# Value projections of a decoder layer: two pairs of groups by seven block products, and eight multiplications of a constant at the start

## The chip, the cores and the metric

The kernel runs on one core of a Trainium2 chip. A core has five engines that run side by side, each with its own queue of instructions, which it works off in order: TensorE (PE in the profile, with its weight loads shown apart as PEld) multiplies matrices into PSUM, VectorE (DVE), ScalarE (ACT) and GpSimd (POOL) work on elements, and SyncE (SP) does nothing here but issue transfers. Sixteen DMA engines move data between HBM and SBUF. The engines wait for each other by semaphores. The metric is the device time of the program in microseconds, from first to last instruction; smaller is better. Everything is computed in float32.

## The reference

One decoder layer over 8 sequences of 112 tokens with 512 features: causal self-attention with 16 heads of 128, linear cross-attention to a context, and a mixture of eight experts of which each token takes two, each followed by a layernorm. The change touches the self-attention alone:

```python
q = jnp.einsum('bsd,hed->bhse', x, W_Q)
k = jnp.einsum('bsd,hed->bhse', x, W_K)
v = jnp.einsum('bsd,hed->bhse', x, W_V)
scores = jnp.einsum('bhse,bhme->bhsm', q, k) * scale
scores = jnp.where(causal, jnp.float32(-1000000000.0), scores)
pattern = jax.nn.softmax(scores, axis=-1)
z = jnp.einsum('bhsm,bhme->bhse', pattern, v)
out = jnp.einsum('bhse,hde->bsd', z, W_O)
```

## The kernel before

**Tiles.** The 896 tokens are 7 tiles of 128 (`xn`, tokens on the partitions). TensorE turns each tile with four transposes (`transposing`, L199), and VectorE or ScalarE copies the result from PSUM to `xT`, features on the partitions. The weights come as blocks of 1 MB, each for a group of four heads (512 columns), into nine buffers `slab[0]` to `slab[8]`. The names in the profile are `slab`, `xn`, `x0T` (for `xT`), `vps` (PSUM of a value product), `qk_5a` (PSUM of the projections of head 5), `ws` (combined weights), `xs` (combined tokens).

**Seven products.** `seven` (L304) computes two matrix products with the same right side at once. The two weight blocks and the tokens are split in halves, by features (`low`, `high`) and by tokens (sequences 0 to 3 and 4 to 7). Four products of halves for each of the four blocks of the result would be eight; with sums and differences of the halves it is seven. The sums of the weights are ws[0] = w2 low + w2 high, ws[1] = ws[0] - w1 low, ws[2] = w1 low - w2 low, ws[3] = w1 high - ws[1]. The sums of the tokens are made once (`combine_tokens`, L289) and called s1 to s4 below (`xs[:, 0]` to `xs[:, 3]`): three subtractions on VectorE (L293 to L295), s3 on GpSimd (L292). `seven` uses three PSUM banks a, b and c; into a and c products are added on after ScalarE (L328, L332, L335, L339) or VectorE (L330, L336, L342) has read what stood there. Each of the seven is two multiplications of 128 rows.

**Values.** Head group 0 and group 3 have their values projected directly (`project_v`, L344): 8 sequences, four multiplications each, 32 in all. Groups 1 and 2 are done as a pair (`project_v_pair`, L363): four times fourteen multiplications, 56 in all. Group 0 comes first of everything, each sequence as its tile is turned; the pair comes in step h = 4 of the loop over heads, group 3 in step h = 8. `v_buf` holds the values of two groups.

**The loop over heads.** In step h the queries and keys of head h are projected (by `seven`, with its combined weights on GpSimd, L299 to L302), mixed with the transposes and products of head h - 1 (`mix`), followed by the scores of head h and their softmax (`patterns`): scaling on ScalarE (L419), the mask on GpSimd (L425), row maximum (L435) and shift (L436) on VectorE, exponential on ScalarE (L437), row sum (L439), reciprocal and scaling on VectorE. After every fourth head, the output of the group is projected and added to `xn` (L261, L268).

**Order.** The order of the instructions on each engine is set by a scheduler that the program calls on while it is built; what it places depends on its costs, not on the order of the text. Each engine then runs its queue strictly in that order. Loads from SP's queue also stand in order; the program counts the transfers of SP and ScalarE with eight semaphores in turn, so that a ninth transfer waits for the first.

Of the kernel before, what the change touches and what calls it, by code (L numbers as in the profile page):

```python
# [17 lines left out]
ORDERED = {ET.PE, ET.DVE, ET.Activation, ET.SP}  # L18

P = 128  # L20
B, S, D = 8, 112, 512
T = B * S
NT = T // P
# [3 lines left out]
G = 4  # L27
# [33 lines left out]
def decoder_layer(ctx: ExitStack, tc: tile.TileContext, t_in: dict, out: bass.AP):  # L61
# [13 lines left out]
    def bank(name: str, tag: str = "mm"):  # L75
        return psum.tile([P, 512], F32, tag=tag, name=name)
# [3 lines left out]
    def weights(which: str, i: int, at: int):  # L80

        w = slab[at]
        nc.sync.dma_start(out=w.rearrange("p c n -> p (c n)"), in_=t_in[which][i])
        return w
# [1 line left out]

    xe = keep.tile([P, NT, W], F32, tag="xn", name="xn")
    xn = xe[:, :, :D]
    wv0 = slab[0]
    nc.scalar.dma_start(out=xn[:, 0, :], in_=t_in["x"][:P, :])  # L90
    for c in range(C):
        nc.sync.dma_start(out=wv0[:, c, :], in_=t_in["wv"][0][:, c * 512 : (c + 1) * 512])
    for t in range(1, NT):
        nc.sync.dma_start(out=xn[:, t, :], in_=t_in["x"][t * P : (t + 1) * P, :])

    ident = const.tile([P, P], F32, name="ident")
    make_identity(nc, ident)
# [39 lines left out]
    for half in range(2):  # L137
# [5 lines left out]
            allow_small_or_imprecise_dtypes=True,  # L143
        )
    place.append(pairs_.rearrange("p i q e -> p (i q) e"))
    nc.gpsimd.iota(
        xe[:, :, XK],
        pattern=[[P, NT]],
        base=0,
        channel_multiplier=1,  # L150
        allow_small_or_imprecise_dtypes=True,
    )

    upto = counting("upto", [P, NT + 1, E], [[0, NT + 1], [T, E]])

# [40 lines left out]
                in_=blank[:, :D].unsqueeze(1).broadcast_to([P, 2 * NT + 1, D]),  # L196
            )

    def transposing(xT, name: str):  # L199

        for t in range(NT):
            ps = bank(f"{name}_ps{t}")
            for c in range(C):
                nc.tensor.transpose(
                    ps[:, c * P : (c + 1) * P], xn[:, t, c * P : (c + 1) * P], ident
                )
            src = ps.rearrange("p (c n) -> p c n", c=C)
            if t % 2:
                nc.scalar.copy(xT[:, :, t * P : (t + 1) * P], src)
            else:  # L210
                nc.vector.tensor_copy(xT[:, :, t * P : (t + 1) * P], src)  # L211
            yield t
# [57 lines left out]


    xT = keep.tile([P, C, T], F32, tag="xT", name="x0T")
    turned = transposing(xT, "x0T")
    with tc.tile_pool(name="att", bufs=2) as att:


# [9 lines left out]
        )  # L286
        v_buf = [att.tile([S, B, 512], F32, name=f"v{i}", bufs=1) for i in range(2)]

        def combine_tokens():  # L289
            b11, b12 = xT[:, low, :HALF], xT[:, low, HALF:]  # L290
            b21, b22 = xT[:, high, :HALF], xT[:, high, HALF:]
            nc.gpsimd.tensor_sub(xs[:, 2], b22, b12)  # L292
            nc.vector.tensor_sub(xs[:, 0], b12, b11)  # L293
            nc.vector.tensor_sub(xs[:, 1], b22, xs[:, 0])
            nc.vector.tensor_sub(xs[:, 3], b21, xs[:, 1])  # L295

        def combine_weights(out, w1, w2):

# [5 lines left out]
        def seven(name: str, tag: str, w1, w2, ws, cols, turned_: bool, c11, c12, c21, c22):  # L304

            x = [xs[:, i, :, cols] for i in range(4)]
            b11, b21, b22 = xT[:, low, cols], xT[:, high, cols], xT[:, high, HALF:]
            b22 = b22[:, :, cols]
            rows, n = (S, 512) if turned_ else (P, HALF)

            def product(ps, a, b_, start: bool):

                for c in range(C // 2):
                    l, r = (b_, a) if turned_ else (a, b_)
                    nc.tensor.matmul(  # L315
                        ps[:rows, :n],
                        l[:, c, :],
                        r[:, c, :],
                        start=start and c == 0,
                        stop=c == C // 2 - 1,  # L320
                        skip_group_check=not start,
                    )

            e1, e2 = ends[:rows, 0, :n], ends[:rows, 1, :n]
            pa, pb, pc = (bank(f"{name}{i}", tag) for i in "abc")
            u, r, q = (ps[:rows, :n] for ps in (pa, pb, pc))
            product(pa, w1[:, low], b11, True)
            nc.scalar.copy(e1, u)  # L328
            product(pb, w1[:, high], b21, True)
            nc.vector.tensor_add(c11, e1, r)  # L330
            product(pa, ws[1], x[1], False)
            nc.scalar.copy(e2, u)  # L332
            product(pc, ws[0], x[0], True)
            product(pa, ws[2], x[2], False)
            nc.scalar.copy(e1, u)  # L335
            nc.vector.tensor_add(c22, e1, q)  # L336
            yield
            product(pa, w2[:, high], x[3], False)
            nc.scalar.copy(c21, u)  # L339
            yield  # L340
            product(pc, ws[3], b22, False)
            nc.vector.tensor_add(c12, e2, q)  # L342

        def project_v(g: int, w):  # L344
            for b in range(B):
                next(turned, None)
                if b == 1:
                    next(turned, None)
                ps = bank(f"vps_{g}_{b}")
                for c in range(C):  # L350
                    nc.tensor.matmul(  # L351
                        ps[:S, :],
                        xT[:, c, b * S : (b + 1) * S],
                        w[:, c, :],
                        start=(c == 0),
                        stop=(c == C - 1),
                    )
                if b % 2:
                    nc.scalar.copy(v_buf[g % 2][:, b, :], ps[:S, :])
                else:  # L360
                    nc.vector.tensor_copy(v_buf[g % 2][:, b, :], ps[:S, :])

        def project_v_pair(g: int, w1, w2, ws):  # L363

            v1, v2 = v_buf[g % 2], v_buf[(g + 1) % 2]
            pieces = None
            for b in range(B // 2):
                last, pieces = pieces, seven(
                    f"vps_{g}_{b}",
                    ("mm", "aux")[b % 2],  # L370
                    w1,
                    w2,
                    ws,
                    slice(b * S, (b + 1) * S),
                    True,
                    v1[:, b],
                    v1[:, b + B // 2],
                    v2[:, b],
                    v2[:, b + B // 2],
                )  # L380
                for _ in pieces:
                    pass

        def project_qk(h: int, wq, wk, qk):
            hl = slice(h % G * DH, (h % G + 1) * DH)
# [82 lines left out]
                )  # L468
                yield

        project_v(0, wv0)
        combine_tokens()
        at_qk = ((4, 5), (0, 3), (4, 5), (0, 3))
        at_o = (6, 7, 6, 2)
        pats = None
        for h in range(NH + 1):
            g = h // G
            qk = {}
            if h < NH:
                if h % G == 0:  # L480
                    wq, wk = (weights(n, g, i) for n, i in zip(("wq", "wk"), at_qk[g]))
                if h == 0:
                    wv1, wv2 = weights("wv", 1, 1), weights("wv", 2, 2)
                if h == 1:
                    turn_biases()
                if h % G == 2:
                    wo = weights("wo", g, at_o[g])
                if h == 2 * G - 1:
                    wv3 = weights("wv", 3, 1)
                if 2 <= h < E + 3:  # L490
                    clear(h - 2)
            project = project_qk(h, wq, wk, qk) if h < NH else iter(())
            mixed = mix(h - 1, pats) if h else iter(())
            next(project, None)
            next(mixed, None)
            next(project, None)
            next(mixed, None)
            next(mixed, None)
            next(project, None)
            for _ in mixed:  # L500
                pass
            if h < NH:
                pats = patterns(h, qk)
            if h % G == 0 and h:
                if h == G:
                    ws = [slab[i].rearrange("p (a c) n -> p a c n", a=2) for i in (4, 5)]
                    nc.gpsimd.tensor_add(ws[0][:, 0], wv2[:, low], wv2[:, high])
                    nc.gpsimd.tensor_sub(ws[0][:, 1], ws[0][:, 0], wv1[:, low])
                    nc.vector.tensor_sub(ws[1][:, 0], wv1[:, low], wv2[:, low])
                    nc.vector.tensor_sub(ws[1][:, 1], wv1[:, high], ws[0][:, 1])  # L510
                    project_v_pair(1, wv1, wv2, [ws[0][:, 0], ws[0][:, 1], ws[1][:, 0], ws[1][:, 1]])
                elif h == 2 * G:
                    project_v(3, wv3)
                for t in project_and_add(zT, wo, f"ops_{h}"):
                    if h == NH:
                        layernorm(t, "ln1")
# [4 lines left out]
    rb = const.tile([P, E], F32, name="rb")  # L521
    nc.scalar.dma_start(out=rb, in_=t_in["rb"].partition_broadcast(P))
    rows = const.tile([P, NT, 2], I32, name="rows")

    def route(t: int):

# [906 lines left out]
```

## Time and profile before

The median of three runs is 978.79 us (977.5 to 979.02).

| | before |
|---|---|
| median of 3 runs | 978.79 us |
| the profiled execution: its time | 978.09 us |
| its span | 976.5 us |
| matmul records of TensorE | 3915 |
| busy: VectorE / ScalarE / GpSimd | 502.6 / 247.3 / 206.1 us |
| value products of group 0 begin / the first head's projections begin | 7.13 / 40.74 us |
| the h = 4 step's pair begins, head 5's projection begins | 109.21, 188.38 us |
| the h = 8 step's values begin, head 9's projection begins | 240.30, 298.54 us |
| data moved by DMA | 130.48 MB |

A profile is one execution. Its times are positions from the start of its span; the span is shorter than the time by what lies around it (1.6 us). A float32 multiplication stands in it as two records. The times of single matmul records overlap, as they are pipelined, so the distance between their starts counts, not their length. The loads at the start, in 2 us windows: 3, 235, 356, 309, 273, 369, 424, 422, 430 GB/s up to 18 us.

### The profile page before, as it was taken

How to read it: one execution, taken by the hardware profiler on the slowest of the kernel's cores; microseconds unless marked ns; L12 is line 12 of the kernel's file. 1: busy time of each engine (PE TensorE's matmuls, PEld its weight loads, DVE VectorE, ACT ScalarE, POOL GpSimd, SP SyncE). 2: the span in 40 equal slices, each digit the busy share in tenths (PEclk: the TensorE clock that was granted, in tenths of full speed). 3: DMA queues.
4: the chain of work that ended last, by engine and by line, in shares of the span. 5: the costliest groups of instructions: out<-in, count | busy, mean ns of one | idle time of the engine just before them, and what ended most of it. 6: DMA issues, size and time to landing. Idle time of an engine off the chain costs nothing. (4 is left out here: it accounts for less than half of the span.)

```text
span 976.5 us, 11044 instructions
## 1 busy us (share of the span) xinstructions
PE 920.5 (94%) x3915; PEld 467.9 (48%) x3915; DVE 502.6 (51%) x1117; ACT 247.3 (25%) x429; POOL 206.1 (21%) x267
## 2 busy tenths in 40 slices
PE   7998999999999999999999999997969999999981
PEld 3465644466445564664554445454544443334440
DVE  1356521145312552456430756677558864556785
ACT  1133311033102330332322233322224322222232
POOL 3133300021101230302002212212102332222343
PEclk9999999999999999999999999999979999999997
DMA  8995004102011001021100111112356899768953
GB/s 339 348 349 210 1 1 172 44 0 87 1 44 43 1 1 43 1 89 60 32 1 1 32 33 54 54 55 69 143 212 258 282 366 371 270 240 342 386 180 133
DMA packets 35063, 130.48 MB, mean 134 GB/s; under 512 B 3862, under 2 KB 8022, under 8 KB 25152
## 3 DMA queue, kind: packets, MB, share of 16 engines
q1 hardware_dynamic: 29296, 114.01, 32.0%
q0 software_dynamic: 4768, 14.98, 4.3%
q10 hardware_dynamic: 944, 0.79, 0.3%
q8 instruction: 31, 0.51, 0.2%
q14 instruction: 24, 0.20, 0.1%
HBM read 122.02 MB, written 30.06 MB: 156 GB/s over the span
## 5 line engine op out<-in xcount | busy, mean ns | idle before, releaser
L1143 PE MATMUL gups<-slab,bT 128*64 128x512 f32 (+1 forms) x416 | 134.1, 602 | 1.2 <-DMA slab<-in_wu_dram 1.2
L261 PE MATMUL ops<-slab,zT 128*128 128x512 f32 x224 | 97.9, 593 | 0.0
L1143 PEld LDWEIGHTS gups<-slab,bT 128*64 128x64 f32 (+1 forms) x416 | 49.1, 160 | 69.5 <-issue 67.4
L299 POOL TENSOR_TENSOR ws<-slab 128x256 f32<-128x256 f32 x16 | 11.6, 727 | 281.1 <-PE qk_5c L315 83.0
L1172 PE MATMUL yps<-slab,aT 128*64 128x512 f32 (+1 forms) x208 | 68.2, 601 | 0.9 <-ACT aT L1044 0.7
L261 PEld LDWEIGHTS ops<-slab,zT 128*128 128x128 f32 x224 | 42.0, 190 | 50.3 <-issue 49.5
L351 PE MATMUL vps<-slab,x0T 128*112 128x512 f32 x128 | 59.4, 619 | 1.0 <-DVE x0T L211 0.8
L1151 DVE TENSOR_TENSOR gu<-gups,biases 128x512 f32<-128x512 f32 x36 | 24.8, 689 | 59.5 <-PE gups L1143 59.5
L268 DVE TENSOR_TENSOR xn<-xn,ops 128x512 f32<-128x512 f32 x28 | 19.2, 685 | 55.3 <-PE ops L261 55.2
L1044 ACT COPY aT<-aT_ps 128x512 f32<-128x512 f32 x18 | 10.5, 585 | 133.5 <-PE aT_ps L1040 133.4
L1172 PEld LDWEIGHTS yps<-slab,aT 128*64 128x64 f32 (+1 forms) x208 | 24.8, 160 | 37.7 <-issue 35.2
L466 DVE COPY zT<-zps 128x448 f32<-128x448 f32 x32 | 20.0, 624 | 39.8 <-PE zps L459 39.8
L459 PEld LDWEIGHTS zps<-pT,v 112*128 112x128 f32 x256 | 33.5, 192 | 12.3 <-issue 11.2
L351 PEld LDWEIGHTS vps<-slab,x0T 128*112 128x112 f32 x128 | 23.0, 185 | 31.7 <-issue 30.0
L435 DVE TENSOR_REDUCE nm<-p 112x4 f32<-112x448 f32 x32 | 19.7, 615 | 30.5 <-POOL p L425 30.5
L261 PE MATMUL xops<-slab,gate 128*128 128x512 f32 x56 | 27.4, 635 | 7.1 <-DVE gate L870 7.1
L459 PE MATMUL zps<-pT,v 112*128 112x112 f32 x256 | 33.4, 273 | 0.0
L587 POOL DMA_INDIRECT store<-xn,rows x14 | 14.0, 1000 | 82.5 <-DVE count L627 58.8
L1185 POOL DMA_INDIRECT parts<-y,nums x16 | 16.9, 1056 | 62.6 <-DVE y L1183 48.6
L995 DVE STREAM_SHUFFLE biases<-biases 128x1024 f32<-128x1024 f32 (+1 forms) x28 | 30.0, 1104 | 0.0
L419 ACT ACTIVATE p<-sps 112x448 f32<-112x448 f32 x32 | 17.4, 543 | 45.6 <-PE sps L411 45.6
L411 PE MATMUL sps<-k,q 128*112 128x112 f32 x256 | 28.0, 262 | 0.0
(816 smaller groups left out, 1676.6 us busy)
## 6 DMA issues: line engine op xcount, KB each, us to landing
slab<-in_wg_dram SPq DMA_DIRECT2D x26, 1024.0 KB
slab<-in_wu_dram SPq DMA_DIRECT2D x26, 1024.0 KB
slab<-in_wd_dram SPq DMA_DIRECT2D x26, 1024.0 KB
store<-slab SPq DMA_DIRECT2D x8, 1806.0 KB
cT<-in_ctxT_dram SPq DMA_DIRECT2D x8, 750.0 KB
slab<-in_wq_dram SPq DMA_DIRECT2D x4, 1024.0 KB
slab<-in_wk_dram SPq DMA_DIRECT2D x4, 1024.0 KB
slab<-in_wo_dram SPq DMA_DIRECT2D x4, 1024.0 KB
```

Of the source, the lines that this page charges most:

```text
L261: nc.tensor.matmul(ps, aT[:, c, t * P : (t + 1) * P], w[:, c, :], start=(c == 0), stop=(c == C - 1),)
L268: nc.vector.tensor_add(xn[:, t, :], xn[:, t, :], ps)
L351: nc.tensor.matmul(ps[:S, :], xT[:, c, b * S : (b + 1) * S], w[:, c, :], start=(c == 0), stop=(c == C - 1),)
L411: nc.tensor.matmul(ps[:S, i * S : (i + 1) * S], qk["q"][:, rows], qk["k"][:, rows], start=True, stop=True,)
L419: nc.scalar.activation(p.rearrange("s b m -> s (b m)"), ps[:S, :HALF], AF.Copy, scale=1.0 / math.sqrt(DH),)
L435: nc.vector.tensor_reduce(nm, p, AX.X, ALU.max, negate=True)
L459: nc.tensor.matmul(zps[:, i * S : (i + 1) * S], v[:, half * 4 + i, hl * DH : (hl + 1) * DH], pT[:, i * S : (i + 1) * S], start=True, stop= ...
L466: nc.vector.tensor_copy(zT[:, hl, half * HALF : (half + 1) * HALF], zps[:, :HALF])
L995: nc.vector.stream_shuffle(b, b, [0] * XH)
L1143: nc.tensor.matmul(ps[rows_], st["bT"][:, c, rows_], slab[3 * q + k][:, c, :], start=(c == 0), stop=(c == C - 1),)
L1151: nc.vector.tensor_add(a, ps, st["bias"][:, k * I : (k + 1) * I])
L1172: nc.tensor.matmul(ps[rows_], st["aT"][:, c, rows_], slab[3 * q + 2][:, c, :], start=(c == 0), stop=(c == C - 1 and s < STEPS - 1),)
```

## The change

Values of groups 0 and 1 are now a pair at the very start, and groups 2 and 3 a pair in step h = 8; step h = 4 has no value products, and `project_v` is gone. For the first pair both weight blocks are loaded at the start, in halves of 512 KB, and the tiles in the order 0, 1, 3, 4, 5, 2, 6: wv1, tiles 1, 3, 4, 5, then wv2, then tiles 2 and 6. The blocks for the second pair are loaded in step h = 5. `combine_tokens` is called twice, for the first two and the last two of the four batches. The weights of a pair are combined by `combine_values`: on VectorE, only ws[2] of the first pair on GpSimd. The start stands in a block in which the queues of TensorE, VectorE, ScalarE and SP keep the order of the text; GpSimd's is left to the scheduler. At its head TensorE multiplies a tile of ones by itself eight times.

```diff
+    load_tile(0, nc.scalar)
+    for half in range(2):
+        load_half(wv1, 0, half)
+    for t in tiles[1:5]:
+        load_tile(t)
+    for half in range(2):
+        load_half(wv2, 1, half)
+    for t in tiles[5:]:
+        load_tile(t)
...
-            if t % 2:
+            if t % 2 or t and tiles != range(NT):
                 nc.scalar.copy(xT[:, :, t * P : (t + 1) * P], src)
...
             nc.vector.tensor_add(c11, e1, r)
+            if turned_:
+                yield
...
+        def combine_values(w1, w2, at, engine=nc.vector):
+
+            ws = [slab[i].rearrange("p (a c) n -> p a c n", a=2)[:, a] for i in at for a in (0, 1)]
+            nc.vector.tensor_add(ws[0], w2[:, low], w2[:, high])
+            engine.tensor_sub(ws[2], w1[:, low], w2[:, low])
+            nc.vector.tensor_sub(ws[1], ws[0], w1[:, low])
+            nc.vector.tensor_sub(ws[3], w1[:, high], ws[1])
+            return ws
...
-        project_v(0, wv0)
-        combine_tokens()
+        with tc.manual_schedule(engines=ORDERED):
+
+            warm = bank("warm", "aux")
+            for _ in range(8):
+                nc.tensor.matmul(warm[:, :P], allones, allones, start=True, stop=True)
+            turn = lambda n: list(itertools.islice(turned, n))
+            turn(1)
+            ws = [slab[i].rearrange("p (a c) n -> p a c n", a=2)[:, a] for i in (2, 3) for a in (0, 1)]
+            first_values = project_v_pair(0, wv1, wv2, ws)
+            next(first_values[0])
+            turn(2)
+            combine_values(wv1, wv2, (2, 3), nc.gpsimd)
+            next(first_values[1])
+            turn(2)
+            combine_tokens(0, 2 * S)
+            turn(2)
+        for pieces in first_values[:2]:
+            for _ in pieces:
+                pass
+        combine_tokens(2 * S, HALF)
+        for pieces in first_values[2:]:
+            for _ in pieces:
+                pass
...
-                if h == 0:
-                    wv1, wv2 = weights("wv", 1, 1), weights("wv", 2, 2)
...
-                if h == 2 * G - 1:
-                    wv3 = weights("wv", 3, 1)
+                if h == G + 1:
+                    wv1, wv2 = weights("wv", 2, 1), weights("wv", 3, 2)
...
-                if h == G:
-                    ws = [slab[i].rearrange("p (a c) n -> p a c n", a=2) for i in (4, 5)]
-                    nc.gpsimd.tensor_add(ws[0][:, 0], wv2[:, low], wv2[:, high])
-                    nc.gpsimd.tensor_sub(ws[0][:, 1], ws[0][:, 0], wv1[:, low])
-                    nc.vector.tensor_sub(ws[1][:, 0], wv1[:, low], wv2[:, low])
-                    nc.vector.tensor_sub(ws[1][:, 1], wv1[:, high], ws[0][:, 1])
-                    project_v_pair(1, wv1, wv2, [ws[0][:, 0], ws[0][:, 1], ws[1][:, 0], ws[1][:, 1]])
-                elif h == 2 * G:
-                    project_v(3, wv3)
+                if h == 2 * G:
+                    for pieces in project_v_pair(2, wv1, wv2, combine_values(wv1, wv2, (0, 3))):
+                        for _ in pieces:
+                            pass
```

The `iota` that numbers the tokens moves from the head of the program to the text behind the attention. The orders of the queues named in the prediction are those of the two built programs.

More of the change, by code (lines that the diff above doesn't have):

```diff
@@ L88, in decoder_layer, with load_tile, load_half @@
     xn = xe[:, :, :D]
[L89 to L94, printed above, removed]
+    wv1, wv2 = slab[0], slab[1]
+    tiles = (0, 1, 3, 4, 5, 2, 6)
+    def load_tile(t: int, engine=nc.sync):
+        engine.dma_start(out=xn[:, t, :], in_=t_in["x"][t * P : (t + 1) * P, :])
+    def load_half(w, i: int, half: int):
+        at = slice(half * (C // 2), (half + 1) * (C // 2))
+        nc.sync.dma_start(
+            out=w[:, at, :].rearrange("p c n -> p (c n)"),
+            in_=t_in["wv"][i][:, at.start * 512 : at.stop * 512],
+        )
+    load_tile(0, nc.scalar)
[7 more added lines that the diff above has]
+        load_tile(t)
     ident = const.tile([P, P], F32, name="ident")
@@ L145, in decoder_layer @@
     place.append(pairs_.rearrange("p i q e -> p (i q) e"))
[L146 to L152, printed above, removed]
     upto = counting("upto", [P, NT + 1, E], [[0, NT + 1], [T, E]])
@@ L197, in clear, with transposing @@
             )
-    def transposing(xT, name: str):
-        for t in range(NT):
+    def transposing(xT, name: str, tiles=range(NT)):
+        for t in tiles:
             ps = bank(f"{name}_ps{t}")
@@ L272, in decoder_layer @@
     xT = keep.tile([P, C, T], F32, tag="xT", name="x0T")
-    turned = transposing(xT, "x0T")
+    turned = transposing(xT, "x0T", tiles)
     with tc.tile_pool(name="att", bufs=2) as att:
@@ L287, in decoder_layer, with combine_tokens @@
         v_buf = [att.tile([S, B, 512], F32, name=f"v{i}", bufs=1) for i in range(2)]
[L289 to L295, printed above, removed]
+        def combine_tokens(a: int, b: int):
+            b11, b12 = xT[:, low, a:b], xT[:, low, HALF + a : HALF + b]
+            b21, b22 = xT[:, high, a:b], xT[:, high, HALF + a : HALF + b]
+            s1, s2, s3, s4 = (xs[:, i, :, a:b] for i in range(4))
+            nc.gpsimd.tensor_sub(s3, b22, b12)
+            nc.vector.tensor_sub(s1, b12, b11)
+            nc.vector.tensor_sub(s2, b22, s1)
+            nc.vector.tensor_sub(s4, b21, s2)
         def combine_weights(out, w1, w2):
@@ L342, in seven @@
             nc.vector.tensor_add(c12, e2, q)
[L344 to L361, printed above, removed]
         def project_v_pair(g: int, w1, w2, ws):
[L365 to L368, printed above, removed]
+            v1, v2 = v_buf
+            return [
+                seven(
                     f"vps_{g}_{b}",
@@ L380, in project_v_pair @@
                 )
-                for _ in pieces:
-                    pass
+                for b in range(B // 2)
+            ]
         def project_qk(h: int, wq, wk, qk):
@@ L523, in decoder_layer @@
     rows = const.tile([P, NT, 2], I32, name="rows")
+    nc.gpsimd.iota(
+        xe[:, :, XK],
+        pattern=[[P, NT]],
+        base=0,
+        channel_multiplier=1,
+        allow_small_or_imprecise_dtypes=True,
+    )
     def route(t: int):
```

## The prediction

> **What bounds the kernel now.** I read the busy shares first, then the timeline of TensorE, then the timelines of VectorE and GpSimd at the places where TensorE stood still.
>
> ```profile
> PE 920.5 (94%) x3915; PEld 467.9 (48%) x3915; DVE 502.6 (51%) x1117; ACT 247.3 (25%) x429; POOL 206.1 (21%) x267
> ```
>
> TensorE works 94% of the span. The page's chain of waits starts only at 740 us and says nothing of the attention stage, so that stage is read from TensorE's own timeline (start, length, line, records, idle time before):
>
> ```profile
> 5.26 1.09 PE L204 MATMUL x0T_ps<-ident,xn 128*128 128x128 f32 x4 [5.26 <-DMA xn<-in_x_dram]
> 7.13 6.63 PE L351 MATMUL vps<-slab,x0T 128*112 128x512 f32 x8 [0.79 <-DVE x0T L211]
> ...
> 30.44 10.03 PE L351 MATMUL vps<-slab,x0T 128*112 128x512 f32 x23
> 40.74 1.67 PE L315 MATMUL qk_0a<-x0T,slab 128*128 128x448 f32 x4
> ...
> 92.55 1.77 PE L315 MATMUL qk_3a<-xs,ws 128*128 128x448 f32 x4 [2.95 <-ACT slab L332]
> ...
> 247.90 26.77 PE L351 MATMUL vps<-slab,x0T 128*112 128x512 f32 x62
> 274.51 24.20 PE L261 MATMUL ops<-slab,zT 128*128 128x512 f32 x56
> ```
>
> Two things are to be seen. The lines follow each other without idle time, so removed products come off the end time. And the durations overlap: 62 records from 247.90 to 274.51 us are 0.429 us each; a 128x512 product is two records, so **0.858 us**. The first eight records take 6.63 us, 0.85 us each up to about 13.0: half speed, although the granted clock stands at 1.00 there.
>
> The exceptions are a wait of 2.95 us at 92.55 us, and behind it GpSimd:
>
> ```profile
> 17.64 0.72 POOL L299 TENSOR_TENSOR ws<-slab 128x256 f32<-128x256 f32 x1 [12.97 <-DMA slab<-in_wk_dram]
> 31.65 2.99 POOL L292 TENSOR_TENSOR xs<-x0T 128x896 f32<-128x896 f32 x1 [8.50 <-DVE x0T L211]
> ...
> 85.89 2.34 POOL L507 TENSOR_TENSOR slab<-slab 128x1024 f32<-128x1024 f32 x1
> 88.31 2.61 POOL L508 TENSOR_TENSOR slab<-slab,slab 128x1024 f32<-128x1024 f32 x1
> ```
>
> ```profile
> 32.73 2.85 DVE L294 TENSOR_TENSOR xs<-x0T,xs 128x896 f32<-128x896 f32 x1
> 35.62 1.09 DVE L295 TENSOR_TENSOR xs<-x0T,xs 128x896 f32<-128x896 f32 x1
> ...
> 86.08 2.64 DVE L436 TENSOR_TENSOR p<-p,nm 112x448 f32<-112x448 f32 x1
> 89.28 2.12 DVE L436 TENSOR_TENSOR p<-p,nm 112x448 f32<-112x448 f32 x1
> ```
>
> L294 took 2.85 us while L292 ran, its twin L295 took 1.09 us alone; L436 took 2.64 and 2.12 us beside L507 and L508, against 0.62 us in other heads. ScalarE's exponentials and the copy that TensorE waits for came that much later. L299 shows when wk has landed: 17.64 us.
>
> **The change, part by part.** All times are positions in the profiled execution (span 976.5 us, time 978.09 us).
>
> *1. The h = 4 step loses its pair.* 56 products x 0.858 = 48.0 us. One batch takes 12.09 us (131.52 to 143.61) against 28 x 0.429 = 12.01, so four cost 0.3 us of waits more. Sum **-48.3**. Left beside it: head 4's softmax, now under the 24 us of the output projection, as in the h = 12 step before.
>
> *2. The wait at 92.55 us goes.* No value combination runs on GpSimd in head 3 any more: **-2.95**. Nothing is late next there; heads 5 to 7 show the same order without a wait.
>
> *3. The h = 8 step has 56 products for 32.* 24 x 0.858 + 0.3 = **+20.9**.
>
> *4. That pair's combinations all run on VectorE,* inside heads 6 and 7; 1.23 us each for 128x1024 (L510's row). In the changed order of head 7, ws[0] stands between the row maximum (L435) and the shift (L436) of the first half, and the second half's shift falls behind L330's sum (0.53) and L439's row sum (0.58). So the second exponential comes 1.2 + 1.1 - 0.1 = 2.2 us later; the copy queued behind it on ScalarE ended at 223.29, TensorE needs it at 223.74: a stall of 1.75 us. Head 11 confirms the scale: 2.35 us of GpSimd (L709) gave a stall of 1.46. In head 6, ws[2] overwrites a slab that GpSimd reads for head 7's weights until about 203.0, and queued behind it are a zT copy and the row maximum, free to start at 205.05; it finishes 1.15 to 2.3 us too late, less 0.45 of slack, 0.7 to 1.85: I take 1.25, the middle, since either engine may get in first. Together **+3.0** (1.5 to 4). ws[1] and ws[3] fall into idle time (2.3 us before the zT copy at 228.98): nothing.
>
> *5. The start.* Before, value products end at 40.74. Afterwards the same stretch has 56 products and seven transposed tiles, and three inputs can be late.
> - Warm-up: a 128-column record at half speed takes (1.09 - 0.45) / 3 = 0.215 us; 8 products are 16 records, 3.4 us, from the constant (about 1.3) to 4.8, before tile 0 at 5.26. It delays nothing.
> - Loads. Up to 17.64 us 5.47 MB had moved; up to wk the queue held 5.03 MB. Now a further 1.05 MB (wv2) stands ahead of wk: at 0.42 MB/us, wk lands at about 20.1. Cumulated in 2 us windows, wv2 (3.46 MB) lands near 13.5, half of it at 12.4.
> - GpSimd takes ws[2] at 12.4 to 14.7 (2.34, L507). VectorE's three of 1.23 follow, to 18.4, then a sum (0.7) and s1, s2 of the first two batches (half of 1.09 each): 19.5 and 20.1. TensorE has its four products and four more, transposed tiles and copies done at 17.9 to 19.6. Wait: 0 to 1.6 us.
> - Then four products (3.4 us) to 23. The next one needs s3, and s3 is on **GpSimd, behind the weights of head 0**: three L299/L301/L300 and one of head 1, which wait for wk. 20.1 + 4 x 0.69 + half of 1.9 (2.99 less the 1.09 in which L293 held it up) + start = 24.0 if nothing contends. SBUF — State Buffer, section "SBUF: two separate sides", says that a VectorE operation with two SBUF inputs and a GpSimd operation exclude each other and the loser blocks for the whole instruction; four of VectorE's xs subtractions fall into these 4 us. By the rule each of them holds GpSimd up 0.55 us: 26.2. The rows speak for the rule (L294's 2.85), but L508 gave up only 0.3 us of its 2.61. I take 25.3, ends 24.0 and 26.2.
> - From 25.3 on, 56 - 12 = 44 products (eight were made before tile 6, four with s1 and s2): 37.7 + 0.3 of waits: 63.3. Against 40.74: **+22.6**.
>
> TensorE: Matmul & The Clock Gate, "Why this matters for your kernels", asks for 4 us of matmuls ahead of the work. By it the first eight records take 3.4 instead of 6.6 us and the start gains 3 us. By the row of wk it gains nothing: with the old half speed, 7.13 + 6.8 + two tiles and a copy 1.4 + 3.4 + four tiles 2.4 + 3.4 = 24.6, still short of 25.3. I go with the row. The same section wants no idle gaps over 3 us, which speaks against the change: four transposes and a wait, then one of 2.3 us. The row of 92.55 shows full speed after 2.95 us of idleness; a fall is a rival.
>
> *6. Other queues.* SP's wq and wk of group 1 now wait for the value products, to about 62 us; GpSimd wants them after qk_2c, 82 + 22 us. The six store writes move ahead of them: 10.8 MB, 26 us, done by 48. wq of group 3 lands behind wxq, some 40 us before its use. The moved iota costs 0.17 us of idle GpSimd. All hidden; none has less than 20 us of cover.
>
> Sum: -48.3 - 2.95 + 20.9 + 3.0 + 22.6 = **-4.8 us**. What follows attention hangs on its end and shifts as a whole. 978.09 - 4.8 = 973.3; the profiled execution is 0.7 under the median, so the median becomes 974.0, the predicted time. In pure products the change is 8 x 0.858 = 6.9 us; the rest is waits swapped.
>
> **Rivals.**
> - *The start waits less* (chance 0.15): wk lands at 19 and the port costs nothing, so s3 is there at 22.9, with both head stalls at their low ends: -2.4 - 1.5, 970.1. For it: 420 GB/s once the large loads run. Against: L294.
> - *The clock falls back at the start* (0.15): the same page's "Part 4: PE-mode transpose" has it that transposes don't count as activity in the same way (no run here shows it), and 4 us without products precede 19.5. The half-speed stretch before lasted 13.0 - 7.13 = 5.9 us and costs half, 2.9 us: 976.9. No change to be measured, since faster or slower than 0.2% (2.0 us) is what a measurement here can tell. The warm-up not doing its work at all belongs here and costs less.
> - *wk is slowed by the stores* (0.13), the slower side: six store writes of 1.8 MB now come straight behind it, from about 10 us on. Tiles 2, 6 and wq are in at about 17.5; if wk then shares the DMA engines with three stores, its 1.05 MB take 10 us at a quarter of 0.42 MB/us: 27.5. s3 follows 5.2 us behind, and each us of wk beyond 20.1 is one of the total; from 25 on the gain is gone, at 27.5 the time is 981.4. Against it: before, wk landed with only 0.44 MB of later loads moved.
>
> **How the numbers follow.** My forecast has 0.57; its own ends, 24.0 to 26.2 at the start and 1.5 to 4 in the heads, give 971.2 to 975.9. The range reaches to the low rival and past the clock's fall: 969.5 to 979.5; outside it mostly the store rival. Faster: forecast 0.55 of 0.57 and the first rival 0.15: 0.70. Within 0.2%: most of the clock rival and the edge of the others, 0.16. Slower: 0.14.
>
> **What would show it.** The h = 4 output projection right behind the scores; no wait near head 3; stalls of 1 to 2 us on ScalarE's copy in heads 6 and 7; at the start a wait of about 2 us of vps_0a on GpSimd's s3 and GpSimd idle until wk; first vps records 0.43 apart. wk landing past 25 us, or records of 0.85 us after 25 us, would make it wrong.

## The result and the profile after

The changed kernel took **973.18 us** (median of 7 runs, 970.44 to 975.57), the kernel before 978.79 (976.39 to 981.18) on the same chip. The ratio is 0.9947, with a 95% interval of 0.9931 to 0.9963: 5.6 us less by the medians, 3.6 to 6.8 by the interval. The forecast was 974.0. The profiled execution of the changed kernel has a span of 972.7 us and took 974.33, 3.8 less than that of before.

The busy row of the page hardly moves; the eight saved products are 6.9 us, and TensorE's row shows 1.0 of them:

```profile
PE 919.5 (95%) x3915; PEld 468.1 (48%) x3915; DVE 504.3 (52%) x1126; ACT 253.7 (26%) x440; POOL 204.9 (21%) x267
```

The sixteen warm-up records (3.8 us) and products at half clock, which count as busy for longer, are in the same sum. So the page's sums do not explain the result, and the places have to be read one by one. First TensorE's timeline (start, length, engine, line, out<-in, records, idle time before and what ended it):

```profile
5.72 0.65 PE L214 MATMUL x0T_ps<-ident,xn 128*128 128x128 f32 x4 [0.65 <-DMA xn<-in_x_dram]
7.15 1.97 PE L327 MATMUL vps_0a<-slab,x0T 128*112 128x512 f32 x4 [0.78 <-DVE x0T L221]
...
15.47 1.94 PE L214 MATMUL x0T_ps<-ident,xn 128*128 128x128 f32 x16
20.28 2.05 PE L327 MATMUL vps_0c<-slab,xs 128*112 128x512 f32 x2 [2.88 <-DVE xs L305]
22.12 3.62 PE L327 MATMUL vps_0a<-slab,xs 128*112 128x512 f32 x4
25.53 1.38 PE L327 MATMUL vps_0c<-slab,xs 128*112 128x512 f32 x2
26.75 1.88 PE L327 MATMUL vps_0a<-slab,xs 128*112 128x512 f32 x4
...
113.08 1.67 PE L327 MATMUL qk_3a<-xs,ws 128*128 128x448 f32 x4
...
137.26 23.35 PE L271 MATMUL ops<-slab,zT 128*128 128x512 f32 x54
```

Four things are to be seen. The first products are at full speed (four records from 7.15 to 8.95 us). Behind the last transposes TensorE waits 2.88 us for s1. The four products (eight records) that need only s1 and s2 then run at half speed, and the next row, which needs s3, follows at 26.75 without idle time. At 113.08 stands head 3's product for which TensorE waited 2.95 us before: no wait any more. At 137.26 the output projection of h = 4 follows the scores at once, with no value products between.

The helpers at the start, VectorE and then GpSimd:

```profile
15.35 1.23 DVE L468 TENSOR_TENSOR slab<-slab 128x1024 f32<-128x1024 f32 x1 [3.71 <-DMA slab<-in_wv_dram]
16.61 1.23 DVE L470 TENSOR_TENSOR slab<-slab,slab 128x1024 f32<-128x1024 f32 x1
17.86 1.23 DVE L471 TENSOR_TENSOR slab<-slab,slab 128x1024 f32<-128x1024 f32 x1
19.01 0.68 DVE L342 TENSOR_TENSOR v<-slab,vps_1b 112x512 f32<-112x512 f32 x1
19.61 0.62 DVE L305 TENSOR_TENSOR xs<-x0T 128x448 f32<-128x448 f32 x1
...
21.87 1.15 DVE L306 TENSOR_TENSOR xs<-x0T,xs 128x448 f32<-128x448 f32 x1
```

```profile
21.61 0.93 POOL L311 TENSOR_TENSOR ws<-slab 128x256 f32<-128x256 f32 x1 [7.26 <-DMA slab<-in_wk_dram]
22.50 1.10 POOL L313 TENSOR_TENSOR ws<-slab,slab 128x256 f32<-128x256 f32 x1
23.57 1.10 POOL L312 TENSOR_TENSOR ws<-ws,slab 128x256 f32<-128x256 f32 x1
24.63 0.72 POOL L311 TENSOR_TENSOR ws<-slab 128x256 f32<-128x256 f32 x1
25.31 1.13 POOL L304 TENSOR_TENSOR xs<-x0T 128x448 f32<-128x448 f32 x1
```

VectorE stood idle for 3.71 us until wv2 had landed at 15.35. GpSimd stood idle for 7.26 us until wk had landed at 21.61 and made s3 (L304) as its fifth operation from there, finished at 26.44. The same operation of 256 columns takes 0.72 us alone and 1.10 beside VectorE; L306 takes 1.15 instead of 0.62.

To compare whole stages I took one mark in both timelines, the first record of a head's second product (tile qk_Nb; the expectations call it the second-half record), and subtracted. This table is worked out from both timelines:

| mark | before | after | difference | step between |
|---|---|---|---|---|
| qk_0b | 42.25 | 66.46 | +24.21 | start +24.21 |
| qk_3b | 84.92 | 108.57 | +23.65 | small waits of heads 0 to 2, -0.56 |
| qk_4b | 102.81 | 123.25 | +20.44 | head 3 -3.21 |
| qk_5b | 189.89 | 161.95 | -27.94 | h = 4 -48.38 |
| qk_7b | 219.23 | 191.87 | -27.36 | head 6 +0.58 |
| qk_8b | 233.90 | 207.33 | -26.57 | head 7 +0.79 |
| qk_9b | 300.05 | 294.40 | -5.65 | h = 8 +20.92 |
| end | 976.5 | 972.7 | -3.8 | later stages +1.85 |

The attention stage thus ended 5.65 us earlier. Of that, this execution gave back 1.7 us near 545 us, where the granted clock fell to 0.50 for 3.4 us; the execution of before had no fall there. The prediction had taken the later stages to shift as a whole.

### The profile page after: what moved, and what is told of

It reads as the page before. It is cut to its first block, busy times and chain, and to the rows that moved or that the text cites. A ratio compares the mean times of both kernels' runs of the same rounds, so it can differ in the third digit from the quotient of the medians.

```text
span 972.7 us, 11086 instructions
## 1 busy us (share of the span) xinstructions
PE 919.5 (95%) x3915; PEld 468.1 (48%) x3915; DVE 504.3 (52%) x1126; ACT 253.7 (26%) x440; POOL 204.9 (21%) x267
## 5 line engine op out<-in xcount | busy, mean ns | idle before, releaser
L431 ACT ACTIVATE p<-p 112x448 f32<-112x448 f32 x32 | 18.4, 576 | 33.3 <-DVE p L430 32.2
L405 PEld LDWEIGHTS sps<-k,q 128*112 128x112 f32 x256 | 26.6, 178 | 0.5 <-issue 0.4
```

The source lines that it names most:

```text
L405: nc.tensor.matmul(ps[:S, i * S : (i + 1) * S], qk["q"][:, rows], qk["k"][:, rows], start=True, stop=True,)
L431: nc.scalar.activation(p, p, AF.Exp)
```

## Experiments

Theory A is the prediction's sum with one addition from the trace of after: the start ends when s3 does, s3 hangs on wk and on GpSimd's queue, and whatever TensorE does before (a faster first product, a lower clock) disappears in that wait. Each expectation names its rival. Every run has its own comparison with the kernel before; times below are medians, with the range of the runs or the ratio's interval.

**1. The changed kernel without the warm-up products.**

```diff
-            warm = bank("warm", "aux")
-            for _ in range(8):
-                nc.tensor.matmul(warm[:, :P], allones, allones, start=True, stop=True)
```

> The changed kernel without the eight multiplications of the constant. Theory A (the start is set by s3 on GpSimd behind wk): the first eight value records stand 0.85 us apart instead of 0.43 and end about 3.3 us later, TensorE is then less idle before vps_0c, s3 still ends near 26.4 us, and the first head's second projection (qk_0b) stands at 66.5 us within 0.5; time within 1 us of the changed kernel (973.2). Rival B (the warm-up carries the gain): everything behind the first values is 3 us later, qk_0b at 69.5, time 976.

973.15 us (972.06 to 974.65), ratio 0.993 [0.9906, 0.9955]: the same as with them. TensorE's timeline in this kernel:

```profile
5.47 1.09 PE L214 MATMUL x0T_ps<-ident,xn 128*128 128x128 f32 x4 [5.47 <-DMA xn<-in_x_dram]
7.35 3.76 PE L327 MATMUL vps_0a<-slab,x0T 128*112 128x512 f32 x4 [0.78 <-DVE x0T L221]
10.89 1.96 PE L327 MATMUL vps_0b<-slab,x0T 128*112 128x512 f32 x4
...
22.58 1.02 PE L327 MATMUL vps_0c<-slab,xs 128*112 128x512 f32 x2
25.97 1.97 PE L327 MATMUL vps_0a<-slab,xs 128*112 128x512 f32 x4 [2.37 <-POOL xs L304]
```

The first four records are at half speed again and the first eight end 2 us later (12.69 instead of 10.67), but the wait for s3 (2.37 us on GpSimd's L304) takes it all: the product with s3 starts at 25.97, no later than the 26.75 of after. The expected loss of 3.3 us was only 2, as full speed came at 10.9 without any warm-up. By the medians the warm-up is worth nothing in the changed kernel.

**2. Twelve more products of the constant, to fill the wait for s1 and keep the clock up.**

```diff
             turn(2)
+            for _ in range(12):
+                nc.tensor.matmul(warm[:, :P], allones, allones, start=True, stop=True)
```

> The changed kernel with twelve more multiplications of the constant on TensorE between the last transposes and the first product that needs s1 and s2, so that it isn't idle there. Theory A: the clock stays at 1.00 from 17 to 27 us, the four products take 3.4 us instead of 6, and TensorE then waits about 2 us for s3 on GpSimd; qk_0b at 66.5 us within 0.6, time 973. Rival B (the fall of the clock is what sets the start, s3 only seems to): TensorE doesn't wait for s3, qk_0b near 63.7, time 970.4.

974.43 (972.12 to 975.93), 0.995 [0.993, 0.997]. The granted clock stayed at 1.00 up to 544 us, and the product with s3 started at 26.15 after 1.72 us of waiting for GpSimd. A full clock at this place is worth nothing either.

**3 and 4. s3 of the first two batches on VectorE, behind s2; then the same with the twelve products.**

```diff
-        def combine_tokens(a: int, b: int):
+        def combine_tokens(a: int, b: int, third=nc.gpsimd):
...
-            nc.gpsimd.tensor_sub(s3, b22, b12)
             nc.vector.tensor_sub(s1, b12, b11)
             nc.vector.tensor_sub(s2, b22, s1)
+            third.tensor_sub(s3, b22, b12)
...
-            combine_tokens(0, 2 * S)
+            combine_tokens(0, 2 * S, nc.vector)
```

> The changed kernel with s3 of the first two batches on VectorE, behind s2, and no longer on GpSimd behind wk. Theory A (s3 and the clock end together, each hides the other): no wait for GpSimd, but the clock falls to 0.50 near 19 us as before, the four products still end near 26.4, and qk_0b is at 66.2 us within 0.6; time 973. Rival B (s3 alone set the start): ws[2]'s product starts near 24 us, qk_0b near 63.7, time 970.4.

> The changed kernel with both edits: s3 of the first two batches on VectorE, and twelve multiplications of the constant in the gap. Theory A: clock 1.00, no wait for s3, the product with ws[2] starts near 24.3 us instead of 26.5, qk_0b at 64.3 us within 0.5, time 971. Rival B (a third thing, such as ScalarE's copies or the weights of head 0, follows directly behind): qk_0b at 66 us or later, time 973.

971.73 (969.86 to 974.89), 0.9918 [0.9886, 0.995], and 971.57 (971.06 to 972.16), 0.9918 [0.9897, 0.9939]. The product with s3 started at 22.86 and 24.54 instead of 26.75, qk_0b at 62.64 and 64.25. The times alone do not tell these two from the changed kernel, as the intervals overlap; the profiles do. Without the filler I had expected half speed behind the wait, and this was wrong: the wait for s1 was 1.74 us and the clock did not fall. There the rival is right that s3 had set the start, which came even earlier than its 24. What s3 on VectorE is worth when the clock does fall was not seen. The fall is not a fixed part of the program: with nothing changed up to the making of s1, it came at this wait in after (2.88 us) and in number 6 (2.40), and not in number 7 (2.74, where it came at the next wait) or here.

**5. The kernel before with the warm-up products alone.**

```diff
+        warm = bank("warm", "aux")
+        for _ in range(8):
+            nc.tensor.matmul(warm[:, :P], allones, allones, start=True, stop=True)
         project_v(0, wv0)
```

> The kernel before with the eight multiplications of the constant ahead of the first tile, and nothing else of the change. Theory A (there the first products are on the path, nothing later hides them): the first eight value records take 3.4 instead of 6.6 us, qk_0b at 39.2 us instead of 42.25, time 975.8. Rival B (something else at the start takes the place of the half speed, as wk does in the changed kernel): qk_0b above 41.5, time 978.5.

975.29 (974.84 to 980.14, 7 runs) against 978.33, ratio 0.9959 [0.9944, 0.9973]: 3.0 us less. That is the 3 us that the prediction had estimated from the 4 us of matmuls that the Trainium skill asks for in TensorE: Matmul & The Clock Gate, "Why this matters for your kernels" (the sixteen records here take 3.78). That it shows in this kernel because no later input stands behind the first products is argued and not shown by a trace: five of the seven runs took 974.84 to 975.31 us and two 979.71 and 980.14, and the profile is of the run of 979.71, slower than the median of before:

```profile
1.29 3.78 PE L473 MATMUL warm<-allones 128*128 128x128 f32 x16 [1.29 <-DVE allones L127]
5.22 1.09 PE L204 MATMUL x0T_ps<-ident,xn 128*128 128x128 f32 x4
7.09 5.49 PE L351 MATMUL vps<-slab,x0T 128*112 128x512 f32 x8 [0.78 <-DVE x0T L211]
...
91.40 2.13 PE L315 MATMUL qk_3a<-xs,ws 128*128 128x448 f32 x4 [2.97 <-ACT slab L332]
```

Here the transposes still took 1.09 us, as cold, and the first eight records 5.49 us instead of 6.63; full speed came at about 10.9 us, and qk_0b was 1.2 us earlier than before (41.07). Even this part need not be the work of the warm-up, as number 1 reached full speed at 10.9 without it. At 92 us, behind the wait of head 3, the granted clock fell to 0.50 for 3.4 us, which it had not done in the profile of before; from qk_3b to qk_4b this cost 1.7 us. In the profile of after, the same sixteen records brought full speed by 5.7 us (0.65 for the transposes). When the clock rises differs between executions, and seven runs with one profile do not say how often the warm-up works.

**6. ws[0] and ws[1] of the h = 8 pair on GpSimd, the rest on VectorE.**

```diff
-            nc.vector.tensor_add(ws[0], w2[:, low], w2[:, high])
+            first.tensor_add(ws[0], w2[:, low], w2[:, high])
             engine.tensor_sub(ws[2], w1[:, low], w2[:, low])
-            nc.vector.tensor_sub(ws[1], ws[0], w1[:, low])
+            first.tensor_sub(ws[1], ws[0], w1[:, low])
...
-                    for pieces in project_v_pair(2, wv1, wv2, combine_values(wv1, wv2, (0, 3))):
+                    for pieces in project_v_pair(2, wv1, wv2, combine_values(wv1, wv2, (0, 3), nc.vector, nc.gpsimd)):
```

> The changed kernel with ws[0] and ws[1] of the second pair on GpSimd in place of VectorE. Theory A (two-input operations of VectorE and GpSimd exclude each other): head 7's two shifts take over 2 us instead of 0.62, TensorE waits about 2.9 us on ScalarE's copy in head 7, as in head 3 before; heads 6 and 7 lose 3.5 us together instead of 1.4, time 975.3. Rival B (what costs is the place in VectorE's queue): the wait of 0.6 us goes, time 972.6.

976.83 (973.25 to 981.1, 20 runs), 0.9981 [0.9969, 0.9993], above the interval of the changed kernel. From qk_6b to qk_8b it took 33.12 us, after 30.71, and two heads without a stall 29.34: heads 6 and 7 cost 3.8 instead of 1.4 us. GpSimd, VectorE and TensorE in head 7 of this kernel:

```profile
192.19 2.34 POOL L468 TENSOR_TENSOR slab<-slab 128x1024 f32<-128x1024 f32 x1
194.61 2.61 POOL L470 TENSOR_TENSOR slab<-slab,slab 128x1024 f32<-128x1024 f32 x1
```

```profile
192.38 2.63 DVE L430 TENSOR_TENSOR p<-p,nm 112x448 f32<-112x448 f32 x1
194.94 0.61 DVE L429 TENSOR_REDUCE nm<-p 112x4 f32<-112x448 f32 x1
195.58 2.12 DVE L430 TENSOR_TENSOR p<-p,nm 112x448 f32<-112x448 f32 x1
```

```profile
198.85 1.77 PE L327 MATMUL qk_7a<-xs,ws 128*128 128x448 f32 x4 [2.95 <-ACT slab L346]
```

The picture of head 3 before is back, almost to the hundredth: the shifts (L430) take 2.63 and 2.12 us beside GpSimd's two operations, and TensorE waits 2.95 us for ScalarE's copy. So it was GpSimd working on SBUF beside VectorE that cost 2.95 us before, and moving the work to VectorE removes it at a smaller price. One other thing moved with the edit: ScalarE's copy (L346) stands behind both exponentials here, as in head 3 before, and between them in head 7 of the changed kernel.

**7. h = 8 by 64 direct products instead of the pair's 56,** without its combinations.

```diff
-                    for pieces in project_v_pair(2, wv1, wv2, combine_values(wv1, wv2, (0, 3))):
-                        for _ in pieces:
-                            pass
+                    project_v(2, wv1)
+                    project_v(3, wv2)
```

> The changed kernel with groups 2 and 3 projected directly in step h = 8: 64 products and no combined weights in place of 56 and four combinations; the first pair stays. Theory A (the gain is the number of products, each 0.858 us): the h = 8 step is 8 x 0.858 - 0.3 = 6.6 us longer, heads 6 and 7 are 1.4 us shorter, time 973.2 + 5.2 = 978.4. Rival B (the gain is the wait near head 3 and the moved work, not the products): within 2 us of 973.2.

979.63 (976.92 to 982.9, 20 runs), 1.001 [0.9999, 1.0021]. The step from qk_8b to qk_9b took 93.61 us, 6.54 more than after, for 8 products of 0.858 less the pair's 0.3 us of waits. Heads 6 and 7 took 14.67 us each: the combinations cost exactly the 1.37 us of the table. With these products back, nothing is left of the gain: it is a gain of multiplications not done. The time is 1.2 us above the 978.4 that theory A gave. In this profile the clock fell at 25.8 us, behind the wait for s3:

```profile
26.13 3.49 PE L327 MATMUL vps_0a<-slab,xs 128*112 128x512 f32 x4 [2.52 <-POOL xs L304]
```

From here to qk_0b it took 41.33 us, 1.5 more than in number 6 (39.82). A fall behind the last late input is paid for.

**8. s3 on VectorE, and ws[3] behind it,** so that VectorE's s1 comes 1.2 us earlier, with eight filler products. **9 to 11,** measured together on one chip: the changed kernel again, number 8 without the filler, number 8 again. On top of the edits of number 3:

```diff
-            combine_values(wv1, wv2, (2, 3), nc.gpsimd)
+            nc.vector.tensor_add(ws[0], wv2[:, low], wv2[:, high])
+            nc.gpsimd.tensor_sub(ws[2], wv1[:, low], wv2[:, low])
+            nc.vector.tensor_sub(ws[1], ws[0], wv1[:, low])
...
             combine_tokens(0, 2 * S, nc.vector)
+            nc.vector.tensor_sub(ws[3], wv1[:, high], ws[1])
             turn(2)
+            for _ in range(8):
+                nc.tensor.matmul(warm[:, :P], allones, allones, start=True, stop=True)
```

> The changed kernel with s3 of the first two batches on VectorE, ws[3] of the first pair moved behind the first two batches' s1 to s4 on VectorE, and eight multiplications of the constant in the gap. Theory A (the start then hangs on VectorE's chain ws[0], ws[1], s1, s2 behind wv2): the first product with ws[1] starts at 19.7 us, ws[2]'s at 23.1, qk_0b at 63.1 us within 0.6, time 969.8. Rival B (ws[3] is then late for vps_0c, or the clock falls all the same): qk_0b at 64.3 or later, time 971 or more.

> The changed kernel as it is, for a comparison on the same chip with the two runs that follow. Theory A (the start ends when s3 does, GpSimd's five operations behind the landing of wk): again 973.2 within 1. Rival B (what the recorded execution lost to a lower clock near 545 us is typical of this kernel and not of the execution): the fall near 545 is there again and second-half record qk_0b comes near 66.5 as before.

> s3 on VectorE and GpSimd's ws[2] ahead of VectorE's ws[3], without the eight filler products. Theory A: the four products that need no s3 follow one another, so second-half record qk_0b near 62.2 to 62.7 and a median of 970.2 to 970.9, 2.3 to 3.0 below the changed kernel of the same call. Rival C (the eight filler products are what keeps the clock up): a lower clock in the 6 us behind the wait for s1, qk_0b 1.5 to 3.5 us later than with the filler, and a median above the filled kernel's by 1 to 3.

> The same with the eight filler products ahead of the first of the seven products. Theory A: filler is worth nothing, 970.6 within 1, as the kernel without it. Rival C: 1 to 3 below the kernel without it, full clock from 7 to 60 us in this profile only.

| kernel | median us (range, runs) | ratio to before [95%] | product with s3 | qk_0b |
|---|---|---|---|---|
| 8, early, filler | 970.63 (969.57 to 972.09) | 0.9921 [0.9903, 0.9939] | 22.44 | 62.16 |
| 9, the changed kernel | 972.93 (970.89 to 976.82, 6) | 0.9946 [0.9926, 0.9967] | 25.83 | 65.63 |
| 10, early, no filler | **968.12** (967.49 to 971.01, 4) | 0.9899 [0.9882, 0.9917] | 21.50 | 61.27 |
| 11, as number 8 | 971.97 (967.36 to 974.34, 6) | 0.9922 [0.9903, 0.994] | 24.29 | 64.00 |

Number 10 is faster than both kernels: its interval lies below that of number 9, and its start came 4.4 us earlier than in number 9. TensorE in number 10:

```profile
15.36 1.93 PE L214 MATMUL x0T_ps<-ident,xn 128*128 128x128 f32 x16
17.95 1.11 PE L327 MATMUL vps_0c<-slab,xs 128*112 128x512 f32 x2 [0.66 <-DVE xs L304]
18.90 1.88 PE L327 MATMUL vps_0a<-slab,xs 128*112 128x512 f32 x4
20.61 1.02 PE L327 MATMUL vps_0c<-slab,xs 128*112 128x512 f32 x2
21.50 1.94 PE L327 MATMUL vps_0a<-slab,xs 128*112 128x512 f32 x4
```

The wait behind the transposes is 0.66 us for s1, and none is left for s3. A had the products in a row right; its time for number 10 was 2 to 3 us too high. In number 8 the start was 0.9 us earlier than A's 63.1, and the late ws[3] or lower clock of its rival did not come. Number 11 missed A's 970.6 within 1 by 0.4. Rival C, that the filler is needed, is wrong: the product with s3 came later where the eight products were made (by 0.9 us in number 8, by 2.8 in number 11, of which 1.9 are the first four records at half speed). Of rival B of number 9 a part holds: the clock fell again at 543 us, while qk_0b came 0.8 us earlier than in after. It fell near 545 (or 551) in six profiles of kernels with the new start and not in five others, nor in the two with the old one; what decides it is open.

## Why the prediction held, step by step

- **h = 4 loses its pair:** -48.3 predicted, -48.4 measured. **h = 8 gets one:** +20.9 and +20.9. Products at 0.858 us with 0.3 us of waits needed no correction; number 7 shows it from the other side.
- **The wait in head 3:** -2.95 predicted, -3.21 measured. That its cause was GpSimd beside VectorE was argued from L436's rows; number 6 made it come back in another head.
- **Heads 6 and 7: +3.0 predicted, 1.37 measured, the term that was mis-sized** (just under its own low end of 1.5). Head 6 lost 0.58 where I took 1.25 and had 0.7 as the low end. For head 7, where I took 1.75, I had the copy (L346) behind both exponentials on ScalarE and so 2.2 us late. ScalarE's order in the changed kernel has it between them:

```profile
194.75 0.58 ACT L431 ACTIVATE p<-p 112x448 f32<-112x448 f32 x1 [2.15 <-DVE p L430]
195.23 0.51 ACT L346 COPY slab<-qk_7a 128x448 f32<-128x448 f32 x1
196.87 0.58 ACT L431 ACTIVATE p<-p 112x448 f32<-112x448 f32 x1 [1.12 <-DVE rs L434]
```

```profile
198.65 0.57 PE L445 MATMUL pps<-ident,p 112*112 112x112 f32 x4 [0.61 <-DVE p L435]
```

  The copy ends in time, and the late second exponential shows up one step on, as TensorE's 0.61 us for VectorE's normalization (L435). Head 7 lost 0.79 in all. I had looked up the changed order of VectorE and taken ScalarE's from the old one.
- **The start: +22.6 predicted, +24.2 measured.** The chain was the right one: a wait for s1, four products, s3 behind wk. The forecast wait of about 2 us for s3 is not in the profile of after, where slow products filled it, but it is 2.37 us in number 9, the same kernel. wv2 landed at 15.35 instead of 13.5 and s1 was ready at 20.2 instead of 19.5; this vanished in the wait for s3. From the landing of wk to the product with s3 I had 5.2 us, and 5.14 passed (21.61 to 26.75). s3 itself was finished after 4.83 of them, between the 3.9 without contention and the 6.1 that the prediction took if the loser blocks: GpSimd was held up by about 1 us in all, not by 2.2. The term that was mis-sized is the landing of wk, 21.6 instead of 20.1, and not by the rate: by 20.1 us the core had moved 6.5 MB (324 GB/s), just as much as the sum had.

```profile
0.00:20.10 20.10, 14.45 (x60) 9.32 (x60) 6.99 (x13) 5.58 (x9) 5.72 (x22) 0.98 0.88 324
0.00:21.61 21.61, 15.78 (x62) 10.08 (x63) 8.46 (x16) 5.58 (x9) 5.72 (x23) 0.95 0.89 329
```

  (The columns are the stretch, its length, the busy time of PE, PEld, DVE, ACT and POOL, then the granted clock, the DMA share and GB/s.) But wk was complete only when 7.1 MB had moved, 0.6 MB more. The loads up to wk come to 6.1 MB; the prediction had let 0.44 MB of later ones move beside them, as before, and it was 1.0 (the next load in SP's queue is wo). The same holds for wv2, which landed when 4.6 MB had moved (297 GB/s up to 15.35 us) and not 3.46. Why later loads get that far ahead is open. In number 9 wk landed at 20.44 and the start was 0.8 us shorter, so about half of the start's error belongs to the execution. Loading wk ahead of wv2 was not tried. The windows of after around that time, in the same columns:

```profile
18.00:19.00 1.00, 0.00 (x0) 0.00 (x0) 1.00 (x1) 0.16 (x1) 0.00 (x0) 1.00 1.06 434
19.00:20.00 1.00, 0.00 (x0) 0.00 (x0) 1.00 (x3) 0.00 (x0) 0.00 (x0) 0.71 0.99 369
20.00:21.00 1.00, 0.72 (x1) 0.45 (x2) 0.97 (x3) 0.00 (x0) 0.00 (x0) 0.50 0.96 387
...
25.00:26.00 1.00, 1.00 (x2) 0.31 (x1) 0.00 (x0) 0.23 (x1) 1.00 (x2) 0.50 1.07 386
26.00:27.00 1.00, 1.00 (x3) 0.35 (x2) 0.00 (x0) 0.36 (x1) 1.00 (x2) 0.88 1.05 376
```

- **The clock's fall at the start,** which I gave 0.15 and 2.9 us, did happen in the profiled execution: the clock column above reads 0.71, 0.50 and 0.88 from 19 to 27 us. It cost next to nothing, because the four slow products were through just after s3 was finished (26.44; the next row follows at 26.75 without idle time, 0.31 us behind s3, where it came 0.06 behind it in numbers 1, 2 and 9). I had priced it as an addition, though my own row of s3 stood behind it as cover. Numbers 2 and 9 had a full clock there and started with s3 at 26.15 and 25.83, with wk landed at 20.93 and 20.44. That the fall came ahead of s3 and not behind it, as in number 7, was luck.
- **The warm-up:** rule and row gave 3 us against nothing in the changed kernel. The row was right (number 1). In the kernel before the same products bring 3.0 us by the medians (number 5), as the rule would have it, though no trace shows how.
- **The rival with wk behind the stores** did not occur: wk landed between 20.4 and 21.6 us in the profiles read for it (after, numbers 9 and 10). The lighter start (s3 at 22.9) did not occur either.
- **The sum:** -4.8 predicted, -5.65 measured at the end of attention. The errors of +1.6 (start), -0.6 (heads 0 to 2), -0.3 (head 3) and -1.6 (heads 6 and 7) partly cancel, so that the sum is nearer than its terms is luck. By the medians the whole is 5.6.

## What to carry to other kernels

An operation that is ready early but queued behind one that waits for a load comes as late as that load: ask of every input of the next product which engine makes it and what stands ahead there; moving two subtractions here (s3 and ws[3]) was worth 4.8 us by the medians of numbers 9 and 10, beside the 5.6 of the whole change. A faster step ahead of a wait for something else is worth nothing, and a slower one costs nothing as long as it is through before that wait ends, so price warm-up and clock against the input that comes last. A load lands later than the bytes ahead of it in the queue and the rate say, since later loads move beside it (1.0 MB here, where 0.44 was assumed). Read the changed order of every engine of a chain, not only of the one that gets the new work.

## What the runs showed of the hardware

- The granted clock after a short idle time is not one value per program. After 2.88 us of waiting it stood at 0.50 for about 6.8 us in after, after 2.40 us for about 3.4 us in number 6; after 2.74 us (number 7) and 2.37 us (number 9) it stayed at 1.00, and in number 7 it fell behind the next wait, of 2.52 us. Behind head 3's wait it stayed up in the profile of before (2.95 us) and fell in that of number 5 (2.97 us). Ahead of the first wait stand sixteen records of transposes (1.9 us) in after and in numbers 6 and 7; ahead of the waits of 2.52 and 2.97 us stand products. Falls near 545 us lasted about 3.4 us each.
- Sixteen records of 128 columns (3.8 us) ahead of the work brought full speed by 5.7 us in after, but only near 10.9 us in numbers 5, 9 and 11; the four transposes took 0.65 us in the one case and 1.08 to 1.09 in the others. Without them full speed came at 10.9 us in number 1 and at about 13.0 in before. The Trainium skill, TensorE: Matmul & The Clock Gate, "What's actually happening", describes a free-running activity window of about 3.4 us and a number of slow products that varies from run to run; the falls of 3.4 us and the spread of the warm-up agree with that.
- VectorE and GpSimd, both working on SBUF, slow each other in both directions: 256 columns on GpSimd 0.72 us alone and 1.10 beside VectorE, while VectorE's 448 columns rose from 0.62 to 1.15; with GpSimd's 1024 columns, VectorE rose to 2.63.
- Loads queued behind a load move before it is complete: the loads up to wk come to 6.1 MB in after, and 7.1 MB had moved when wk was complete (329 GB/s over 21.61 us); in before 5.0 MB and 5.5 (310 GB/s over 17.64 us).
